# Fourth layer of a graph-network stack: full-array work and weighted values gathered into every second step

## The chip, the core and the metric

The kernel runs on one core of one Trainium2 chip. The metric is the device time of one execution in microseconds (us), lower is better. Engines are named as in the profile: PE is TensorE's matmul stream, PEld its weight loads, DVE is VectorE, ACT is ScalarE, POOL is GpSimd, and SP issues the DMAs. All data are 32-bit floats. One matmul of the program appears as two MATMUL records in the trace.

## The reference, cut to what matters

A stack of four layers works on x of 128 graphs x 64 nodes x 256 features. Each layer adds its result to x. The change touches only the fourth layer, an edge-wise attention over 512 edges with 4 heads:

```
h  = relu(layernorm(x))
Xq = (h @ W_lin.T), Xv = (h @ W_val.T)          # per head 64 wide
e  = einsum(leaky_relu(Xq[:, src] + Xq[:, dst]), a)
e  = e + log(A0[src, dst] + 1e-8)               # A0 is adj, the same for all graphs and heads
attn = softmax of e over the edges that share src
Y  = segment_sum(attn * Xv[:, dst], src)
x  = x + Y @ W_out.T
```

## The kernel before, in words

Three layers come first and take the greater part of the run; they are not touched, apart from one line of the preparation. `layer3` (L2411) is the fourth layer. x lies in SBUF as 16 blocks of 512 rows (8 graphs). A **step** g handles half a block, 4 graphs; there are 32 steps, and 8 steps make a **group** (32 graphs x 4 heads = 128 rows of attention). What follows uses a letter for each kind of PE work:

- **T**, `turned` (L2466): layer norm of the next block (`norm`, four ACT activations that write `h`), then 8 transposes into two PSUM banks. `move` (L1487) copies one bank to `hT` by DVE and the other by ACT, in turn. DVE then makes the sums `hS` that a Strassen-like product needs.
- **Q**, `queries` (L2496): 14 products of 128x256, which give `Q` and the values `V` (called `XV` in the trace). They use four banks (a, b, f, d). The second half is `rest()`; the last copies are ACT's `Q[:, 0:2]` and DVE's `Q[:, 2:4]`. `linear` (L2530) then runs `lin_p` and two reductions on DVE.
- **S**, `score` (L2545): eight products of 64x128 weights with 512 columns, each into a bank of its own. ACT applies relu to each bank, into one of eight `r` tiles.
- **R**, `reduce` (L2558): eight products that add the `r` tiles into one bank `acc` for the whole group.
- **L**: in the first step of a group, one product with a single row, `ones` by `logA`, that starts `acc` with the logarithm of the adjacency.
- **M**, `summed` (L2638), in the last step of a group: one product that adds the linear part to `acc`. `softmax` and `shifted` (L2626, L2642) are then a chain of DVE scans with an exponential on ACT. **E**, in `edgewise` (L2654): four transposes of the softmax, in step 8q+1.
- **G**, `between`/`gathered` (L2666, L2682), ten steps behind the score (`LAG`): DVE makes four `aw` tiles (five buffers), eight products of 128x64 weights write one bank, ACT copies it to `an`.
- **W**, `weighted` (L2693), one step behind G: 16 products of 64x64. DVE and ACT each copy a half to `y`.
- **O**, `output` (L2709): four products with W_out into one bank; DVE adds it to x, and SP sends it out.
- **B**, `back` (L2222), in steps 0 to 7 only: eight transposes that hand blocks 8 to 15 of the third layer's result back into x. They read `ls_t`, a tile with one buffer, whose halves DVE and ACT copy; DVE adds the two banks to x.

S uses PE as tiles of 64x128, R and G as 128x64, W as 64x64; T, Q, O, M, E and B use the full 128x128 array, and these are called **F** together. Before the change every step has the order S, W, R, G, F: T and O in even steps, Q and O in odd steps, with B in steps 0 to 7. The products S, T, Q, O, G, B and E share one pool of five PSUM banks (`l3ps`, all its tiles are called `ps`); a product into a bank waits until the reader of that bank's previous content has finished. `acc` and the output of W have banks of their own.

The order on each engine is fixed when the program is built: a scheduler interleaves the instructions of DVE and ACT, and each engine then follows its own list. Which bank and which predecessor each product gets is fixed with it. All matmuls, copies and activations have the line of a recording helper, L799, so that the trace is read by tiles. `turn` (L2571) is the end of the layer, with an order written out by hand: the last ten steps of G, W and O.

Of the kernel before, what the change touches and what calls it, by code (L numbers as in the profile page):

```python
# [8 lines left out]
F32 = mybir.dt.float32  # L9
I32 = mybir.dt.int32  # L10
AF = mybir.ActivationFunctionType
ALU = mybir.AluOpType
# [6 lines left out]
FLOOR = 1e30  # L19
# [823 lines left out]
class Plan:  # L843
# [56 lines left out]
    def rest(self):  # L900

        while any(self.queue.values()):
            for e in self.queue:
                self.fill(e, 1e9)
# [538 lines left out]
B, N, D = 128, 64, 256  # L1443
P = 128
# [3 lines left out]
E = 512  # L1448
HEADS = 4
NG = 4  # L1450
# [15 lines left out]
class Kernel:  # L1466
# [865 lines left out]
    def edges(self, w, pool, psum):  # L2332


        nc, o, io = self.nc, self.o, self.io
# [58 lines left out]
        ga = cmp[:N, :]  # L2394
        o.mul(ga, p[:N, :], self.OD[:N, :])
        p = psum.tile([P, E], F32, name="pe")
        self.mm(p[0:1, :], self.ones[:N, 0:1], ga)
        self.logA = w.tile([1, E], F32, name="ed_log")
        eps = pool.tile([1, 1], F32, name="ed_eps")
        nc.vector.memset(eps[:], 1e-8)  # L2400
        self.act(self.logA[:], p[0:1, :], AF.Ln, bias=eps[:])

        ac = self.columns(pool, "ed_ac", io["L3_gnn_a"].rearrange("h d -> (h d)"))
        self.apad = w.tile([P, 2, P], F32, name="ed_apad")
# [6 lines left out]
    def layer3(self):  # L2411
        nc, o, io = self.nc, self.o, self.io
        cx, (w,) = self.stage([("l3x", 1)], "tile")
        with cx:
            cy, pools = self.stage([("l3", 2), ("l3v", 2), ("l3s", 1), ("l3r", 6), ("l3ps", 5), ("l3cps", 1), ("l3yps", 1)], "tile")
            with cy:
                self.a02 = self.everywhere(w, "ed_a", io["L3_gnn_a"].rearrange("h d -> (h d)"))
                o.ts(self.a02[:], self.a02[:], 0.2, ALU.mult)
                self.drop, self.dropr = (w.tile([P, E], F32, name="ed_" + n) for n in ("drop", "dropr"))
                o.ts(self.drop[:], self.cont[:], 1.0, ALU.subtract, FLOOR, ALU.mult)  # L2420
                o.ts(self.dropr[:], self.contr[:], 1.0, ALU.subtract, FLOOR, ALU.mult)
                WQV = w.tile([P, 2, 2 * D], F32, name="w3_qv")
                for x, n in enumerate(("W_lin", "W_val")):
                    nc.sync.dma_start(WQV[:, :, x * D:(x + 1) * D],
                                      io[f"L3_gnn_{n}_t"].rearrange("(k p) m -> p k m", p=P))
                WO = self.weights(w, "w3_o", io["L3_gnn_W_out_t"])


                st, LAG = {}, 10
                self.turned(st, 0, *pools)  # L2430
                WQV = self.sums3(w, WQV)
                self.queries(st, 0, WQV, *pools)()
                for g in range(8 * NG):
                    v = g - LAG
                    ahead = (g + 1) // 2 if g % 2 and g + 1 < 8 * NG else None
                    self.score(st, g, *pools)
                    if v >= 1:
                        self.weighted(st, v - 1, *pools)
                    self.reduce(st, g, *pools)
                    if g % 8 == 1 and 1 < g:  # L2440
                        self.edgewise(st, g // 8 - 1, *pools)
                    if v >= 0:
                        self.between(st, v, *pools)
                    if g % 8 == 7 and g + 1 < 8 * NG:
                        self.summed(st, g // 8, *pools)
                    if g < 8:
                        self.back(8 + g, pools[4], "ps")
                    if ahead:
                        rest = self.queries(st, ahead, WQV, *pools)
                    elif g + 2 < 8 * NG:  # L2450
                        self.turned(st, g // 2 + 1, *pools)
                    if g + 6 == 8 * NG:

                        p = pools[4].tile([P, BT], F32, name="ps")
                        for c in range(4):
                            self.nc.tensor.transpose(p[:N, c * P:(c + 1) * P], self.OST[:, c, :], self.ident[:])
                        self.act_copy(self.cont[:N, :], p[:N, :])
                    if v >= 1 and g + 1 < 8 * NG:
                        self.output(st, v - 1, WO, *pools)
                    if ahead:  # L2460
                        rest()
                    if g % 8 == 7 and g + 1 < 8 * NG:
                        self.softmax(st, g // 8, *pools)
                self.turn(st, WO, pools)

# [92 lines left out]
    def reduce(self, st, g, pool, vp, sp, rp, psum, psc, psy):  # L2558


        q, i = g // 8, g % 8
        if i == 0:
            st["acc", q] = psc.tile([P, E], F32, name="acc")
            self.mm(st["acc", q][:], self.ones[0:1, :], self.logA[:], True, False)
        for fc in range(2):
            for k in range(4):
                z = 64 - 32 * (k // 2) - 4 * i
                x = 64 * (k % 2)
                self.mm(st["acc", q][x:x + 64, :], self.apad[:, fc, z:z + 64], st["r"][4 * fc + k][:], False, False)

    def turn(self, st, WO, pools):  # L2571

# [4 lines left out]
        W = [self.spread(st, v, c, *pools) for c in (0, 2)]  # L2577
        self.summed(st, q, *pools)
        e, m, m2 = self.shifted(st, q, *pools)
        self.output(st, v - 2, WO, *pools)  # L2580
        self.gathered(st, v, W, *pools)
        et = m2[:].rearrange("p (c b) -> p c b", c=4)
        p = psum.tile([P, 4, P], F32, name="ps")
        for c in range(4):
            nc.tensor.transpose(p[:, c, :], e[:, c * P:(c + 1) * P], self.ident[:])
        self.act_copy(et, p[:])
        self.weighted(st, v - 1, *pools)
        W = [self.spread(st, v + 1, 0, *pools)]
        p = psum.tile([P, P], F32, name="ps")
        for c in range(4):  # L2590
# [15 lines left out]
                o.mul(at[:, :, x, :, m, :], by(et), by(p))  # L2606
        self.gathered(st, v + 1, W, *pools)
        W = [self.spread(st, v + 2, 0, *pools)]
        self.weighted(st, v, *pools)

        late = lambda: None
        for v in range(8 * NG - 8, 8 * NG + 2):
            if v < 8 * NG:
                W.append(self.spread(st, v, 2, *pools))
            late()
            if v < 8 * NG:
                self.gathered(st, v, W, *pools)
            if v + 1 < 8 * NG:
                W = [self.spread(st, v + 1, 0, *pools)]
            if v <= 8 * NG:  # L2620
                self.weighted(st, v - 1, *pools)
            late = self.output(st, v - 2, WO, *pools, late=True)
        late()
        nc.ordered = False
# [17 lines left out]
    def shifted(self, st, q, pool, vp, sp, rp, psum, psc, psy):  # L2642

        nc, o, acc = self.nc, self.o, st["acc", q]
        e, m, m2 = (vp.tile([P, E], F32, name="sm_" + x, bufs=1) for x in ("e", "m", "m2"))
        scan = nc.vector.tensor_tensor_scan
        scan(m[:], self.drop[:], acc[:], -FLOOR, op0=ALU.add, op1=ALU.max)
        scan(m2[:, ::-1], self.dropr[:, ::-1], acc[:, ::-1], -FLOOR, op0=ALU.add, op1=ALU.max)
        o.tt(m[:], m[:], m2[:], ALU.max)
        o.sub(e[:], acc[:], m[:])  # L2650
        self.act(e[:], e[:], AF.Exp)
        return e, m, m2

# [36 lines left out]
        a = st["a", g] = vp.tile([P, 2, HEADS, N], F32, name="an")  # L2690
        self.act(a[:], A[:], AF.Copy)

    def weighted(self, st, g, pool, vp, sp, rp, psum, psc, psy):  # L2693

        a, V = st["a", g], st["V", g // 2]

        yp = psy.tile([P, 2, E], F32, name="y2")
        for m in range(2):
            for h in range(HEADS):
                for x in range(2):  # L2700
                    s, z = slice(64 * x, 64 * x + 64), slice(64 * (h % 2), 64 * (h % 2) + 64)
                    f = (2 * m + h // 2) * N
                    self.mm(yp[z, x, f:f + N], V[s, 2 * (g % 2) + m, h * N:(h + 1) * N], a[s, m, h, :])
        y = st["y", g] = vp.tile([P, 2, 2, 2, N], F32, name="y", bufs=3)
        for x in range(2):
            (self.move if g < 8 * NG - 11 else self.act_copy)(y[:, :, :, x, :].rearrange("p f m s -> p m f s"),
                      yp[:, x, 0:4 * N].rearrange("p (m f s) -> p m f s", m=2, f=2))

    def output(self, st, g, WO, pool, vp, sp, rp, psum, psc, psy, late=False):  # L2709

        y = st["y", g]
        out = self.io["out"].rearrange("b n d -> (b n) d")
        parts = []
        for lo, hi in ((0, 1), (1, 2)) if g == 8 * NG - 1 else ((0, 2),):
            p = psum.tile([P, 2, D], F32, name="ps")[:, 0:hi - lo, :]
            for m in range(lo, hi):
                for f in range(2):
                    self.mm(p[:, m - lo, :], y[:, f, m].rearrange("p x s -> p (x s)"), WO[:, f, :], f == 0, f == 1)
            parts.append((p, lo, hi))

        def add():
            for p, lo, hi in parts:
                x = self.X[g // 2][:, 2 * (g % 2) + lo:2 * (g % 2) + hi, :]
                self.o.add(x, x, p)
                self.nc.sync.dma_start(out[(2 * g + lo) * P:(2 * g + hi) * P, :].rearrange("(t p) d -> p t d", p=P), x)

        if late:
            return add
        add()
# [57 lines left out]
```

## Time and profile before

| what | value |
|---|---|
| median of 3 runs | 2326.25 us (2324.82 to 2326.69) |
| span of the profiled execution, first to last instruction | 2325.1 us |
| the median above that span | 1.15 us |
| granted TensorE clock | 0.997 |
| first S of the fourth layer | at 1755.30 us |
| last S (step 31) | at 2239.21 us |
| steps 18 and 19, S to S (2019.66 to 2053.41) | 33.75 us |
| PE busy in 1980 to 2115 us, of 135 us | 134.66 us |
| DVE and ACT busy there | 90.34 us and 55.86 us |

The profiled execution has no time of its own beside its span. A block's duration is taken from its first start to the next block's first start, since matmul ends are modelled and overlap. A PE that counts as busy can still be stretched: the same eight products of S take 3.84 us in one step and 4.91 us in another. A chain of waits names, at each step, what released an instruction last.

### The profile page before, as it was taken

The page shows a single profiled execution, that of the slowest core. Times are in us where ns is not written, and L with a number is a line of the kernel's source. Part 1 is how long each engine was busy: PE and PEld are TensorE (multiplying, and loading weights), DVE is VectorE, ACT ScalarE, POOL GpSimd, SP SyncE. Part 2 cuts the span into 40 slices and gives each one's busy share as a digit, 9 for nine tenths or more (in the row PEclk, how much of TensorE's full clock was granted, in tenths as well). Part 3 has the DMA queues.
Part 4 walks back from the last instruction along what each step waited for, and adds up shares of the span by engine and source line. Part 5 has one row for each costly group of instructions (what it writes and reads, how often), then busy time and mean ns, then how long its engine had stood idle before and what let it go on. Part 6 is the DMA issues. An engine that isn't in the chain of part 4 may idle for free.

```text
span 2325.1 us, 32725 instructions
## 1 busy us (share of the span) xinstructions
PE 2283.6 (98%) x12169; PEld 1633.1 (70%) x12169; DVE 1629.3 (70%) x4054; ACT 1139.5 (49%) x2483; POOL 3.0 (0%) x26
## 2 busy tenths in 40 slices
PE   7999998999999999999999999999999999999999
PEld 4554445676777788888999998888885544554544
DVE  8887676888447777666767676559756686766667
ACT  5765865754436654433444444336435544444321
POOL 0000000000000000000000000000000000000000
PEclk9999999999999999999999999999999999999999
DMA  5000211230000000001000002000010000000001
GB/s 171 1 1 26 65 56 30 71 83 19 1 37 0 1 19 1 1 1 37 1 1 1 1 1 73 1 1 17 1 46 28 1 5 15 15 19 14 14 24 46
DMA packets 61065, 54.81 MB, mean 24 GB/s; under 512 B 15203, under 2 KB 58724, under 8 KB 60900
## 3 DMA queue, kind: packets, MB, share of 16 engines
q1 hardware_dynamic: 60900, 52.66, 7.4%
q8 instruction: 97, 1.59, 0.3%
q14 instruction: 68, 0.56, 0.1%
HBM read 35.86 MB, written 16.78 MB: 23 GB/s over the span
## 4 chain that ended last, share of the span: by engine, by line
PE 79%; DVE 3%; issue 1%; ACT 1%; DMA 0%; SPq 0%; ACTq 0%; DVEq 0%
PE ps L799 69%; PE acc L799 5%; PE pt L799 4%; PE pe L799 1%; PE y L799 1%; DVE aw L799 1%; DVE X L799 1%; DVE sm_m L799 0%; DVE XV L799 0%; ACT ls_g L799 0%; ACT h L799 0%; DVE ls_g L799 0%; ACT big L799 0%; DVE ls_t L799 0%; DVE sm_e L799 0%
## 5 line engine op out<-in xcount | busy, mean ns | idle before, releaser
L799 ACT ACTIVATE ls_g<-ls_g,ls_b 128x512 f32<-128x512 f32 (+4 forms) x472 | 243.1, 565 | 151.4 <-DVE ls_g L799 149.6
L799 ACT ACTIVATE ls_g<-ps,ls_b 128x256 f32<-128x256 f32 (+3 forms) x268 | 115.5, 470 | 330.9 <-PE ps L799 327.7
L799 PE MATMUL ps<-z,w 128*128 128x512 f32 x512 | 254.9, 621 | 0.9 <-ACT z L799 0.9
L799 PE MATMUL ps<-big,X 128*128 128x176 f32 (+3 forms) x848 | 212.7, 366 | 0.1
L799 DVE TENSOR_TENSOR ls_g<-ls_z,ps 128x512 f32<-128x512 f32 (+5 forms) x256 | 146.8, 579 | 91.9 <-PE ps L799 90.4
L799 DVE TENSOR_TENSOR aw<-at,ed_OST 128x1024 f32<-128x1024 f32 x128 | 149.9, 1219 | 83.0 <-PE ps L799 82.8
L799 PE MATMUL ps<-ls_tx,X 128*128 128x160 f32 (+2 forms) x960 | 206.8, 326 | 0.6 <-ACT ls_g L799 0.6
L799 PE MATMUL ps<-X,X 128*128 128x160 f32 (+1 forms) x896 | 199.1, 306 | 0.0
L799 PE MATMUL ps<-X,ls_w 128*128 128x256 f32 x640 | 190.5, 379 | 0.0
L799 PEld LDWEIGHTS ps<-ls_tx,X 128*128 128x128 f32 x960 | 161.8, 190 | 15.1 <-DVE X L799 4.8
L799 PEld LDWEIGHTS ps<-big,X 128*128 128x128 f32 x848 | 145.9, 190 | 29.7 <-issue 19.4
L799 DVE TENSOR_TENSOR X<-ls_g 128x1024 f32<-128x1024 f32 (+2 forms) x108 | 117.4, 1087 | 49.9 <-ACT ls_g L799 49.8
L799 ACT ACTIVATE r<-ps 128x512 f32<-128x512 f32 x256 | 131.6, 614 | 41.5 <-PE ps L799 41.4
L799 PEld LDWEIGHTS ps<-X,X 128*128 128x128 f32 x896 | 148.4, 190 | 0.0
L799 PE MATMUL ps<-X,ls_s 128*128 128x256 f32 x480 | 142.3, 379 | 0.0
L799 PEld LDWEIGHTS ps<-z,w 128*128 128x128 f32 x512 | 87.2, 190 | 69.0 <-issue 60.2
L799 PE MATMUL ps<-ls_tx,ls_s 128*128 128x256 f32 x464 | 134.8, 379 | 0.0
L799 PE MATMUL ps<-ed_S,Q 64*128 64x512 f32 x512 | 132.9, 618 | 1.4 <-DVE hT L799 0.7
L799 PE MATMUL ps<-ls_tx,ls_w 128*128 128x256 f32 x464 | 133.2, 380 | 0.0
L799 PEld LDWEIGHTS ps<-X,ls_w 128*128 128x128 f32 x640 | 121.4, 190 | 16.8 <-DVE X L799 0.3
L799 PE MATMUL ps<-big,ls_w 128*128 128x256 f32 x464 | 131.9, 379 | 0.7 <-ACT ls_z L799 0.7
L799 PE MATMUL ps<-aw,ed_ODT 128*64 128x512 f32 x512 | 117.3, 595 | 0.1
(545 smaller groups left out, 4019.0 us busy)
## 6 DMA issues: line engine op xcount, KB each, us to landing
X<-in_x_dram SPq DMA_DIRECT2D x32, 512.0 KB
xs<-X SPq DMA_DIRECT2D x16, 512.0 KB
X<-xs SPq DMA_DIRECT2D x16, 512.0 KB
out_dram<-X SPq DMA_DIRECT2D x31, 256.0 KB
X<-in_L_gnn_Wih_t_dram SPq DMA_DIRECT2D x4, 512.0 KB
ls_w<-in_L_gnn_Wih_t_dram SPq DMA_DIRECT2D x4, 512.0 KB
ls_w<-in_L_gnn_Whh_t_dram SPq DMA_DIRECT2D x4, 512.0 KB
w<-in_L_gnn_W_t_dram SPq DMA_DIRECT2D x2, 512.0 KB
```

The source lines that it names most:

```text
L799: i = method(*a, **kw)
```

## The change

In the main loop, the full-array work F is done only after odd steps; there it holds (in steps 1, 3, 5, 7) both B, then Q, then two O, the rest of Q, and T for the block after the next. W is done only in even steps, for the two steps before, into one PSUM tile and one `y` tile (two buffers instead of three); its copies are 128x512 instead of 128x256, half as many. M and E move into F of the odd step. T of block 1 goes ahead of the loop. L is gone: `logA` is now held on all 128 partitions, the first `reduce` product of each half starts `acc`, and `shifted` begins with one DVE addition `e = acc + logA`; the scans and the subtraction then read `e` from SBUF. `turn` has three O at its start instead of one.

```
@@ preparation of the edges
-        self.mm(p[0:1, :], self.ones[:N, 0:1], ga)
-        self.logA = w.tile([1, E], F32, name="ed_log")
+        self.mm(p[:], self.ones[:N, :], ga)
+        self.logA = w.tile([P, E], F32, name="ed_log")
@@ layer3
+                self.turned(st, 1, *pools)
                 for g in range(8 * NG):
-                    v = g - LAG
-                    ahead = (g + 1) // 2 if g % 2 and g + 1 < 8 * NG else None
+                    v, odd, last = g - LAG, g % 2, g + 1 == 8 * NG
                     self.score(st, g, *pools)
-                    if v >= 1:
-                        self.weighted(st, v - 1, *pools)
+                    if last:
+                        self.weighted(st, [v - 1], *pools)
+                    elif v >= 2 and not odd:
+                        self.weighted(st, [v - 2, v - 1], *pools)
                     self.reduce(st, g, *pools)
+                    if v >= 0:
+                        self.between(st, v, *pools)
+                    if not odd or last:
+                        continue
+                    if g % 8 == 7:
+                        self.summed(st, g // 8, *pools)
                     if g % 8 == 1 and 1 < g:
                         self.edgewise(st, g // 8 - 1, *pools)
...
                     if g < 8:
-                        self.back(8 + g, pools[4], "ps")
-                    if ahead:
-                        rest = self.queries(st, ahead, WQV, *pools)
-                    elif g + 2 < 8 * NG:
-                        self.turned(st, g // 2 + 1, *pools)
+                        for i in (7 + g, 8 + g):
+                            self.back(i, pools[4], "ps")
+                    rest = self.queries(st, (g + 1) // 2, WQV, *pools)
...
-                    if v >= 1 and g + 1 < 8 * NG:
-                        self.output(st, v - 1, WO, *pools)
-                    if ahead:
-                        rest()
+                    for u in (v - 3, v - 2):
+                        if u >= 0:
+                            self.output(st, u, WO, *pools)
+                    rest()
+                    if g + 3 < 8 * NG:
+                        self.turned(st, (g + 3) // 2, *pools)
@@ reduce
-            self.mm(st["acc", q][:], self.ones[0:1, :], self.logA[:], True, False)
@@ turn
-        self.output(st, v - 2, WO, *pools)
+        for u in (v - 4, v - 3, v - 2):
+            self.output(st, u, WO, *pools)
@@ shifted
-        scan(m[:], self.drop[:], acc[:], -FLOOR, op0=ALU.add, op1=ALU.max)
-        scan(m2[:, ::-1], self.dropr[:, ::-1], acc[:, ::-1], -FLOOR, op0=ALU.add, op1=ALU.max)
+        o.add(e[:], acc[:], self.logA[:])
+        scan(m[:], self.drop[:], e[:], -FLOOR, op0=ALU.add, op1=ALU.max)
+        scan(m2[:, ::-1], self.dropr[:, ::-1], e[:, ::-1], -FLOOR, op0=ALU.add, op1=ALU.max)
         o.tt(m[:], m[:], m2[:], ALU.max)
-        o.sub(e[:], acc[:], m[:])
+        o.sub(e[:], e[:], m[:])
@@ weighted
+        yp = psy.tile([P, 2, 2, 4, N], F32, name="y2")
+        y = vp.tile([P, 2, 4, 2, N], F32, name="y", bufs=2)
+        for k, g in enumerate(gs):
...
+        n = 2 * len(gs)
         for x in range(2):
-            (self.move if g < 8 * NG - 11 else self.act_copy)(y[:, :, :, x, :].rearrange("p f m s -> p m f s"),
+            (self.move if gs[-1] < 8 * NG - 11 else self.act_copy)(y[:, :, 0:n, x, :], yp[:, x, :, 0:n, :])
```

The built order of the changed kernel is, from step 12 on, for an even step e and the odd step o after it: S(e), W (64 records in place of 32, for two steps), R, G, S(o), R, G, then F as Q, O, O, rest of Q, T, and S of the next even step right behind T.

More of the change, by code (lines that the diff above doesn't have):

```diff
@@ L2396, in edges @@
         p = psum.tile([P, E], F32, name="pe")
-        self.mm(p[0:1, :], self.ones[:N, 0:1], ga)
-        self.logA = w.tile([1, E], F32, name="ed_log")
-        eps = pool.tile([1, 1], F32, name="ed_eps")
+        self.mm(p[:], self.ones[:N, :], ga)
+        self.logA = w.tile([P, E], F32, name="ed_log")
+        eps = pool.tile([P, 1], F32, name="ed_eps")
         nc.vector.memset(eps[:], 1e-8)
-        self.act(self.logA[:], p[0:1, :], AF.Ln, bias=eps[:])
+        self.act(self.logA[:], p[:], AF.Ln, bias=eps[:])
         ac = self.columns(pool, "ed_ac", io["L3_gnn_a"].rearrange("h d -> (h d)"))
@@ L2432, in layer3 @@
                 self.queries(st, 0, WQV, *pools)()
+                self.turned(st, 1, *pools)
                 for g in range(8 * NG):
-                    v = g - LAG
-                    ahead = (g + 1) // 2 if g % 2 and g + 1 < 8 * NG else None
+                    v, odd, last = g - LAG, g % 2, g + 1 == 8 * NG
                     self.score(st, g, *pools)
-                    if v >= 1:
-                        self.weighted(st, v - 1, *pools)
+                    if last:
+                        self.weighted(st, [v - 1], *pools)
+                    elif v >= 2 and not odd:
+                        self.weighted(st, [v - 2, v - 1], *pools)
                     self.reduce(st, g, *pools)
+                    if v >= 0:
[4 more added lines that the diff above has]
+                        self.summed(st, g // 8, *pools)
                     if g % 8 == 1 and 1 < g:
                         self.edgewise(st, g // 8 - 1, *pools)
[L2442 to L2445, printed above, removed]
                     if g < 8:
-                        self.back(8 + g, pools[4], "ps")
-                    if ahead:
-                        rest = self.queries(st, ahead, WQV, *pools)
-                    elif g + 2 < 8 * NG:
-                        self.turned(st, g // 2 + 1, *pools)
-                    if g + 6 == 8 * NG:
+                        for i in (7 + g, 8 + g):
+                            self.back(i, pools[4], "ps")
+                    rest = self.queries(st, (g + 1) // 2, WQV, *pools)
+                    if g == 8 * NG - 5:
                         p = pools[4].tile([P, BT], F32, name="ps")
@@ L2457, in layer3 @@
                         self.act_copy(self.cont[:N, :], p[:N, :])
-                    if v >= 1 and g + 1 < 8 * NG:
-                        self.output(st, v - 1, WO, *pools)
-                    if ahead:
-                        rest()
-                    if g % 8 == 7 and g + 1 < 8 * NG:
+                    for u in (v - 3, v - 2):
[4 more added lines that the diff above has]
+                        self.turned(st, (g + 3) // 2, *pools)
+                    if g % 8 == 7:
                         self.softmax(st, g // 8, *pools)
@@ L2568, in reduce @@
                 x = 64 * (k % 2)
-                self.mm(st["acc", q][x:x + 64, :], self.apad[:, fc, z:z + 64], st["r"][4 * fc + k][:], False, False)
+                self.mm(st["acc", q][x:x + 64, :], self.apad[:, fc, z:z + 64], st["r"][4 * fc + k][:],
+                        i == 0 and fc == 0 and k < 2, False)
     def turn(self, st, WO, pools):
@@ L2586, in turn @@
         self.act_copy(et, p[:])
-        self.weighted(st, v - 1, *pools)
+        self.weighted(st, [v - 1], *pools)
         W = [self.spread(st, v + 1, 0, *pools)]
@@ L2608, in turn @@
         W = [self.spread(st, v + 2, 0, *pools)]
-        self.weighted(st, v, *pools)
+        self.weighted(st, [v], *pools)
         late = lambda: None
@@ L2620, in turn @@
             if v <= 8 * NG:
-                self.weighted(st, v - 1, *pools)
+                self.weighted(st, [v - 1], *pools)
             late = self.output(st, v - 2, WO, *pools, late=True)
@@ L2691, in gathered, with weighted @@
         self.act(a[:], A[:], AF.Copy)
[L2693 to L2704, printed above, removed]
+    def weighted(self, st, gs, pool, vp, sp, rp, psum, psc, psy):
+        yp = psy.tile([P, 2, 2, 4, N], F32, name="y2")
+        y = vp.tile([P, 2, 4, 2, N], F32, name="y", bufs=2)
+        for k, g in enumerate(gs):
+            a, V = st["a", g], st["V", g // 2]
+            st["y", g] = y, 2 * k
+            for m in range(2):
+                for h in range(HEADS):
+                    for x in range(2):
+                        s, z = slice(64 * x, 64 * x + 64), slice(64 * (h % 2), 64 * (h % 2) + 64)
+                        self.mm(yp[z, x, h // 2, 2 * k + m, :], V[s, 2 * (g % 2) + m, h * N:(h + 1) * N], a[s, m, h, :])
+        n = 2 * len(gs)
         for x in range(2):
-            (self.move if g < 8 * NG - 11 else self.act_copy)(y[:, :, :, x, :].rearrange("p f m s -> p m f s"),
-                      yp[:, x, 0:4 * N].rearrange("p (m f s) -> p m f s", m=2, f=2))
+            (self.move if gs[-1] < 8 * NG - 11 else self.act_copy)(y[:, :, 0:n, x, :], yp[:, x, :, 0:n, :])
     def output(self, st, g, WO, pool, vp, sp, rp, psum, psc, psy, late=False):
-        y = st["y", g]
+        y, k = st["y", g]
         out = self.io["out"].rearrange("b n d -> (b n) d")
@@ L2717, in output @@
                 for f in range(2):
-                    self.mm(p[:, m - lo, :], y[:, f, m].rearrange("p x s -> p (x s)"), WO[:, f, :], f == 0, f == 1)
+                    self.mm(p[:, m - lo, :], y[:, f, k + m].rearrange("p x s -> p (x s)"), WO[:, f, :], f == 0, f == 1)
             parts.append((p, lo, hi))
```

## The prediction

> **What bounds the kernel now.** First the page's engine line and the chain of work that ended last:
>
> ```profile
> PE 2283.6 (98%) x12169; PEld 1633.1 (70%) x12169; DVE 1629.3 (70%) x4054; ACT 1139.5 (49%) x2483; POOL 3.0 (0%) x26
> ...
> PE 79%; DVE 3%; issue 1%; ACT 1%; DMA 0%; SPq 0%; ACTq 0%; DVEq 0%
> ```
>
> PE works nearly always, and the chain is PE. So the time is the sum of the lengths of PE's blocks, and two things can change it: the number of products, and what lengthens a block without showing as idle time. I read block lengths in the timeline, from first start to first start. Steps 18 and 19, PE alone:
>
> ```profile
> 2033.90 3.97 PE L799 MATMUL ps<-ed_S,Q 64*128 64x512 f32 x16
> 2037.80 0.69 PE L799 MATMUL y<-an,XV 64*64 64x64 f32 x32
> 2038.42 3.65 PE L799 MATMUL acc<-r,ed_apad 128*64 128x512 f32 x16
> 2041.91 3.60 PE L799 MATMUL ps<-aw,ed_ODT 128*64 128x512 f32 x16
> 2045.44 1.13 PE L799 MATMUL ps<-w_qv,hT 128*128 128x256 f32 x4
> 2046.41 1.89 PE L799 MATMUL ps<-w_t,hS 128*128 128x256 f32 x8
> 2049.00 1.89 PE L799 MATMUL ps<-w_o,y 128*128 128x256 f32 x8
> ...
> 2053.41 3.91 PE L799 MATMUL ps<-ed_S,Q 64*128 64x512 f32 x16
> ```
>
> An odd step's S takes 3.90, W .62, R 3.49, G 3.53, then 7.97 for Q and O. Eight S products behind one another need about .43 each, 3.5 in all; the rest is a wait for a free bank, since ACT's relu comes every .504 ("r x8, 4.03"). In a step whose S stands directly behind T, it is longer:
>
> ```profile
> 1812.46 1.09 PE L799 MATMUL ps<-ident,ls_t 128*128 128x128 f32 x8
> 1813.15 1.28 DVE L799 TENSOR_TENSOR X<-X,ps 128x512 f32<-128x512 f32 x2 [3.91 <-PE ps L799]
> ...
> 1814.35 4.98 PE L799 MATMUL ps<-ed_S,Q 64*128 64x512 f32 x16
> 1814.66 0.58 ACT L799 ACTIVATE hT<-ps 128x512 f32<-128x512 f32 x1
> 1814.95 0.60 DVE L799 COPY ls_t<-big 128x512 f32<-128x512 f32 x1
> 1815.14 0.59 ACT L799 ACTIVATE h<-X,n_m,n_r 128x256 f32<-128x256 f32 x1
> 1815.63 0.58 ACT L799 ACTIVATE r<-ps 128x512 f32<-128x512 f32 x1
> 1816.11 0.59 ACT L799 ACTIVATE h<-X,n_m,n_r 128x256 f32<-128x256 f32 x1
> 1816.60 0.59 ACT L799 ACTIVATE r<-ps 128x512 f32<-128x512 f32 x1
> ```
>
> This S lasts 4.92, to R's start at 1819.27. ACT first copies `hT`, then alternates `h` and relu, so banks come free every .97 instead of every .50. In steps 1, 3, 5 and 7 that costs 1 us each.
>
> **What goes.** Each term is a difference of block lengths in this one execution; its span is 2325.1, 1.15 below the median of the runs (no other time of it is shown), and I add the sum to the median 2326.25.
>
> 1. L: 1.05 in steps 8, 16, 24; in step 0 it lies beside a wait for `hT`. −3.15. The four DVE additions in its place stand in the softmax chain, which has whole steps of room; in the last group 3.5 us more of O stand ahead of E.
> 2. W: the 32 records span .47 (8 groups of four, 58 ns apart) of .62, so .15 to .16 is entry and exit. Ten merged pairs: −1.6. In steps 16 and 24 W is split around L (.37 + .50), .25 more each: −.5.
> 3. F once in two steps. Leaving full-array work costs about .09 (O is 1.82 before S, 1.73 before Q), entering .06 to .10 (T .93 against .87 pure). Sixteen times .15: −2.4. The new neighbours (R or G directly before S) are not shown; the rows nearest, the last product of G (.52 for .42) and the first of S (.53 for .42), price them at what S, W, R already pay, so 0; ends −.1 and +.1 each, ±1.6 in all.
> 4. E moved into F, steps 17 and 25: R 3.59, E .59 and G 3.58 shrink by about .3: −.6. Small edges at steps 0 and 9: −.4.
> 5. S of the sixteen odd steps now follows G (or R) with no T or O before it, and with ACT free. The first relu starts 1.16 after S, then every .50; the last product waits only for the third relu, 2.75 + .06 after S, and R comes 3.77 after S. Sum 16 × 3.77 = 60.3 against 68.9 (eleven or so at 3.9, four at 4.9, 5.5 in step 9): −8.6.
>
> Together −17.3. The eviction rule of the Trainium skill speaks against 5: "TensorEngine Tiling (Array Packing)", section "PSUM Bottleneck", says that tiling speeds TensorE but not the emptying of PSUM, which may become the bottleneck. By it each S would last eight relus, 4.03, and term 5 would be −4.4, the time 4.2 later. The row of S(18), 3.84 with five banks to run ahead in, decides for the smaller price.
>
> **What comes.**
>
> 6. S of the even steps. Before, O stood between T and S:
>
> ```profile
> 2031.15 1.09 PE L799 MATMUL ps<-ident,h 128*128 128x128 f32 x8
> ...
> 2032.08 1.89 PE L799 MATMUL ps<-w_o,y 128*128 128x256 f32 x8
> ...
> 2032.28 0.60 ACT L799 ACTIVATE hT<-ps 128x512 f32<-128x512 f32 x1 [0.39 <-PE ps L799]
> 2032.77 2.06 ACT L799 ACTIVATE h<-X,n_m,n_r 128x256 f32<-128x256 f32 x4
> ```
>
> ACT had done `hT` and the four `h` (to 2034.83) when the first S product was ready for it (2035.12). Now T stands directly ahead of S in every even step up to 28, as in steps 1 to 7 above: ACT's `hT` begins about .16 after S, and in its built order the four `h` alternate with relus. The relus start 1.16, 2.13 and 3.10 after S; the product behind the third starts at 3.7 and needs 1.05 to R when it is alone (1818.21 to 1819.27). That alone makes S 4.8.
>
> A second hold: the last S products take T's banks, one of which DVE's `hT` copy frees. That copy stands in DVE's order behind the tail of Q: the last `Q` copy starts .20 after the last products of Q (2052.65), then `lin_p` .79, `XV` 1.15, the reductions .59 later, 2.42 for both: 4.95. The last Q group starts .86 + .97 before S now, so `hT` runs from 3.3 to 4.0 after S, and the product comes at 4.06: S is 5.1. The trace shows the same hold once, in step 9:
>
> ```profile
> 1867.82 0.68 DVE L799 COPY hT<-ps 128x512 f32<-128x512 f32 x1
> ...
> 1868.56 0.30 PEld L799 LDWEIGHTS ps<-ed_S,Q 64*128 64x128 f32 x4 [1.57 <-DVE hT L799]
> ```
>
> By built order the copy is late in steps 0, 4, 6, 12, 14, 20, 22, 28 (5.1 each: 40.8), earlier in 2, 8, 10, 18, 26 (4.8: 24.0); in 16 and 24 the softmax scans delay it further, about 5.8 (11.6). Sum 76.4 against 59.3 in those fifteen steps: +17.1. Bounds: 0 where R's and ACT's room hid it all, 28 if DVE made every one 5.8.
>
> 7. Second B of steps 1, 3, 5, 7. `ls_t` has one buffer, and its refill by DVE stands behind both `X` additions of the first B: the first starts B + .69 and the second ends B + 1.97 (rows above), the copy takes .60, so the second B starts at B + 2.56 instead of B + .87: 4 × 1.69 = +6.8. Below: 0 if ACT's and DVE's copies were made early. Scans in step 7: +.3.
>
> Steady F has no new stall by the rows: `aw` is five buffers ahead as before and DVE has the same work per pair of steps; the W copies are half as many, beside PE. SP's DMAs stay two in a pair, later by a step; nothing waits for them but the end, whose last ten steps keep their order.
>
> Sum: −17.3 + 17.1 + 6.8 + .3 = +6.9, so **2333**.
>
> **Rivals.** (a) *Even S isn't held*: relus keep up, banks come free as now, S stays 3.84. For it: in even steps ACT was done in time, and the pool has three banks that T doesn't use. Against it: the S of 1814.35 behind T. It gives 2333.2 − 17.1 = 2316, faster; it decides from the point where S of the even steps is below 3.95 + (17.3 − 7.1)/15 = 4.6, where gain and loss cancel with B's price kept. (b) *The second B isn't late*: `ls_t` is filled while Q's wait lasts elsewhere; 2333.2 − 6.8 = 2326, no change. (c) *VectorE later*: the `hT` copy, held by a backlog, makes almost every even S 5.8 as in 16 and 24: fifteen steps 87 against 76.4, 2340 to 2342 with the bounds of 3. For it: DVE is busy two thirds of the time and F now brings T's and Q's DVE work in one heap; against it: it has two steps to clear. That the change does not do what it says is excluded by the built order: L is absent and W's 64 records stand in a row.
>
> **How the numbers follow.** Forecast 2333, with 2329 to 2338 as its own range (term 3's ends, term 6 by .2 us a step): 62%, mostly slower (52), partly within 0.2% (10). Rival (a) 13%: faster 11, same 2. Rival (b) 10%: same 8, one each side. Rival (c) 15%: slower. Sums: faster .12, same .20, slower .68; 0.2% (4.65 us, 2321.6 to 2330.9) is about what a measurement of this kernel can tell from no change. The range goes from 2322, which leaves out most of (a), to 2342, which takes in (c).
>
> **What would show it.** In the profile after: S of even steps 4.8 to 5.1 with `h` rows between the relus of ACT and weight loads waiting for DVE `hT`; odd S about 3.8; the second B 2.5 us behind the first; no row of `ones` by `ed_log`; W in 64 records of about 1.1. If even S is near 3.9, or the second B follows at .9, terms 6 or 7 were wrong; if odd S is near 4.0, term 5 was; if R, G and W blocks are longer beside their new neighbours, term 3 was.

## The result and the profile after

The changed kernel takes 2343.29 us (median of 5 runs, 2339.79 to 2346.30) against 2326.25 (median of 5 runs, 2324.82 to 2329.14): ratio 1.0064, 95% interval 1.0051 to 1.0077. It is **slower by 17 us**; the forecast was 7 us slower. The ratio stands for 15 us (12 to 18 by its interval), less than the quotient of the two medians, 1.0073: the kernel before, run again on four later occasions (7 to 29 executions each), had medians of 2327.72 to 2328.45, 1.5 to 2.2 above the five here. The profiled execution of the changed kernel has a time of 2346.30 and a span of 2344.5, 19.4 longer than the span of before. The page's engine line:

```profile
PE 2294.2 (98%) x12161; PEld 1645.4 (70%) x12161; DVE 1629.4 (70%) x4048; ACT 1139.5 (49%) x2473; POOL 2.9 (0%) x26
```

DVE and ACT are as busy as before, to 0.1 us, PE has eight records fewer, and its busy time is 10.6 us longer. The chain of waits is PE's again, 80% for 79%. Nothing in these views names a cause: PE's blocks have become longer inside. So the whole layer was added up by kind of block, start to start, from the first T (1742.89 before, 1746.57 after) to the last O (2317.82 and 2337.28):

| blocks of the fourth layer | predicted, us | before, after | measured |
|---|---|---|---|
| L (term 1) | -3.15 | 3.15, 0 | -3.15 |
| W (term 2) | -2.1 | 13.62, 11.54 | -2.08 |
| T, Q, O, E, G, start and tail (terms 3 and 4) | -3.4 | 300.50, 297.46 | -3.04 |
| R | 0 | 112.89, 115.05 | +2.16 |
| S of odd steps (term 5) | -8.6 | 68.89, 66.70 | -2.19 |
| S of even steps 0 to 28 (term 6) | +17.1 | 59.24, 76.78 | +17.54 |
| B (term 7, with the 0.3 of step 7) | +7.1 | 7.38, 13.91 | +6.53 |
| sum, with unlisted blocks that did not change | +6.9 | 574.94, 590.72 | +15.8 |

The 3.7 us that the span has beyond these lie ahead of the layer, where the granted clock between 100 and 200 us was 0.97 in this execution and 1.00 in that of before. A kernel below with the same code up to there (both O behind T) starts the layer at 1741.25 with a clock of 0.998, so they are not the change's. The five spans of the changed kernel go from 2338.0 at a clock of 0.998 to 2344.5 at 0.995.

**An even S after** (step 14, timeline; T ends, S begins):

```profile
1962.17 1.04 PE L799 MATMUL ps<-ident,h 128*128 128x128 f32 x8
...
1963.14 5.24 PE L799 MATMUL ps<-ed_S,Q 64*128 64x512 f32 x16
1963.24 0.60 ACT L799 ACTIVATE hT<-ps 128x512 f32<-128x512 f32 x1 [2.00 <-PE ps L799]
...
1964.04 2.43 DVE L799 TENSOR_REDUCE lin<-lin_p 64x16 f32<-64x1024 f32 x2
1964.30 0.60 ACT L799 ACTIVATE r<-ps 128x512 f32<-128x512 f32 x1
1964.79 0.59 ACT L799 ACTIVATE h<-X,n_m,n_r 128x256 f32<-128x256 f32 x1
...
1966.51 0.69 DVE L799 COPY hT<-ps 128x512 f32<-128x512 f32 x1
...
1968.30 1.16 PE L799 MATMUL y<-an,XV 64*64 64x64 f32 x64
```

S lasts 5.16, from 1963.14 to W at 1968.30. ACT does `hT`, then `h` and relu in turn; DVE's `hT` copy, which frees a bank, comes 3.4 us after S began, behind the two reductions: the row that the forecast built by hand. The second B, in the waits view and in the timeline of step 1:

```profile
PEld ps L799 <- DVE ls_t L799: 6.8, 4, 1.7
```
```profile
1776.49 1.28 DVE L799 TENSOR_TENSOR X<-X,ps 128x512 f32<-128x512 f32 x2 [10.40 <-PE ps L799]
...
1777.69 0.61 DVE L799 COPY ls_t<-big 128x512 f32<-128x512 f32 x1
...
1778.36 1.09 PE L799 MATMUL ps<-ident,ls_t 128*128 128x128 f32 x8 [1.47 <-DVE ls_t L799]
```

The columns of the first are the total, the times and the longest: four waits of at most 1.7 us, 6.8 in all; the first B began at 1775.80, so the second is 2.56 behind it.

**What was not foreseen** is step 9:

```profile
1876.61 3.35 DVE L799 RECIPROCAL sm_m<-sm_m 128x512 f32<-128x512 f32 x1
...
1876.90 2.99 PE L799 MATMUL ps<-ed_S,Q 64*128 64x512 f32 x12
...
1878.12 0.60 ACT L799 ACTIVATE r<-ps 128x512 f32<-128x512 f32 x1 [2.50 <-PE ps L799]
...
1878.73 1.28 ACT L799 ACT_TABLE_LOAD   x1
...
1881.82 0.20 ACT L799 ACTIVATE n_y<-n_v 128x4 f32<-128x4 f32 x1 [1.80 <-DVE n_v L799]
1881.93 2.53 ACT L799 ACTIVATE r<-ps 128x512 f32<-128x512 f32 x5
1882.56 0.98 PEld L799 LDWEIGHTS ps<-ed_S,Q 64*128 64x128 f32 x4 [3.50 <-ACT r L799]
```

In ACT's fixed order, layer norm's square root `n_y` with its table load stands behind the first relu of S. Its input `n_v` comes from DVE, which is in the softmax's reciprocal until 1879.96 and does six smaller operations before `n_v` starts at 1881.61. For 3.8 us no relu starts, the five banks fill, and PE's weight loads wait 3.50 us. S takes 8.15, R behind it 5.68 (before: 5.50 and 3.77).

### The profile page after: what moved, and what is told of

Read it like the earlier page. It is cut to its first block, busy times and chain, and to the rows that moved or that the text cites. A ratio compares the mean times of both kernels' runs of the same rounds, so it can differ in the third digit from the quotient of the medians.

```text
span 2344.5 us, 32706 instructions
## 1 busy us (share of the span) xinstructions
PE 2294.2 (98%) x12161; PEld 1645.4 (70%) x12161; DVE 1629.4 (70%) x4048; ACT 1139.5 (49%) x2473; POOL 2.9 (0%) x26
## 4 chain that ended last, share of the span: by engine, by line
PE 80%; DVE 3%; ACT 1%; issue 1%; DMA 0%; ACTq 0%; DVEq 0%; SPq 0%
PE ps L799 69%; PE acc L799 5%; PE pt L799 4%; PE pe L799 1%; PE y L799 1%; DVE X L799 1%; DVE sm_m L799 0%; ACT ls_g L799 0%; ACT h L799 0%; DVE lin L799 0%; DVE ls_t L799 0%; DVE aw L799 0%; DVE ls_g L799 0%; DMA ed_a<-in_L_gnn_a_dram 0%; DVE XV L799 0%
## 5 line engine op out<-in xcount | busy, mean ns | idle before, releaser
L799 PE MATMUL ps<-ed_S,Q 64*128 64x512 f32 x512 | 146.7, 627 | 2.9 <-ACT r L799 2.7
L799 PE MATMUL acc<-r,ed_apad 128*64 128x512 f32 x512 | 119.5, 608 | 0.0
```

Source lines behind the costliest of these rows:

```text
L799: i = method(*a, **kw)
```

## Experiments

Theory A: an even S is held twice, by ACT's `h` among the relus and behind that by the bank that DVE's `hT` copy frees late. B: ACT alone. C: T directly ahead of S costs PE by itself. The three kernels are the changed one, each with an order added (`hold` puts what follows behind a given instruction in the built order of its engine; all diffs below are shortened):

```diff
 # late_h: ACT's four h behind the relus of the even step
+        self.nc.hold((None, None, behind))      # behind = last relu of the even S
         for j in range(TPB):
             self.act(h[:, j, :], self.X[i][:, j, :], AF.Relu, ...)
+        self.nc.hold()
 # early_hT: linear called behind T, ordered behind DVE's hT copy
-            self.linear(st, i, ...)              # at the end of rest()
+                    nc.hold((None, st["copied"], None))
+                    self.linear(st, (g + 1) // 2, *pools)
+                    nc.hold()
 # both_orders: both edits
```

> The changed kernel, with ACT's four h activations ordered behind the eight relus of the even step's S; nothing else. Theory A (the even S is held twice: first by ACT, which alternates h and relu, and behind that by T's bank, which DVE's hT copy frees late): the relus come every .50, but S stays near 5.1 in the steps 0, 4, 6, 12, 14, 20, 22, 28 and 5.8 in 16 and 24, where the bank is late anyway; only 2, 8, 10, 18, 26 fall from 4.8 to about 3.9. The sum of the fifteen falls by about 4, the time by about 4 us. Theory B (ACT alone holds it): all fifteen fall to about 3.9, the time by 15 to 17 us. Theory C (T directly ahead of S costs PE by itself, whatever ACT and DVE do): no change.

> The changed kernel, with DVE's lin_p and its two reductions ordered behind the hT copy of T; nothing else. Theory A: T's bank is free about 1.2 us after S begins, and what is left is ACT's alternation: all fifteen even S about 4.8, the sum falls from 76.8 to 72, the time by 4 to 5 us. Theory B (ACT alone): no change in S. Theory C: no change.

> The changed kernel with both orders: h behind the relus on ACT, linear behind the hT copy on DVE. Theory A: fifteen even S of 3.85 to 3.9, sum 58 in place of 76.8, the time 16 to 19 us lower: far more than the two single edits add up to (8 to 9), since either hold suffices. Theory B: the same as late_h. Theory C: no change in S.

| kernel | fifteen even S, us | odd S, us | layer without its start, us | time, us |
|---|---|---|---|---|
| before | 59.24 | 68.89 | 562.5 | 2326.25 |
| changed | 76.78 | 66.70 | 577.9 | 2343.29 |
| late_h | 74.62 | 67.86 | 575.8 | 2343.57 |
| early_hT | 70.78 | 67.84 | 572.8 | 2339.74 |
| both_orders | 59.27 | 71.25 | 564.9 | 2332.15 |

(The start, up to the first S, is left out of the fourth column: it was 12.78 in the profiles of the changed kernel and of best, and 11.2 in seven others that have the same work there. The kernel before, run beside the last three, took 2328.45; their ratios to it are 1.0070, 1.0050 and 1.0017.) Alone the edits give 2.2 and 6.0 us of even S, together 17.5. B and C fall, A stands. Its sum for late_h was missed by half: S of step 2 rose to 5.17, 18 and 26 are 4.21, and S of step 9 grew to 9.31; the layer is 2.1 shorter and the time no lower. Step 14 of late_h, timeline:

```profile
1960.71 3.91 PE L799 MATMUL ps<-ed_S,Q 64*128 64x512 f32 x14
...
1961.87 3.53 ACT L799 ACTIVATE r<-ps 128x512 f32<-128x512 f32 x7 [0.46 <-PE ps L799]
...
1964.08 0.69 DVE L799 COPY hT<-ps 128x512 f32<-128x512 f32 x1
...
1964.82 1.12 PE L799 MATMUL ps<-ed_S,Q 64*128 64x512 f32 x2 [0.21 <-DVE hT L799]
```

Seven relus run in a row, and the last product still waits for `hT`; S is 5.17 as in the changed kernel. The same step of both_orders:

```profile
1955.06 3.91 PE L799 MATMUL ps<-ed_S,Q 64*128 64x512 f32 x16
...
1956.22 4.03 ACT L799 ACTIVATE r<-ps 128x512 f32<-128x512 f32 x8 [0.46 <-PE ps L799]
```

S is 3.84. But the time fell by 11, not 16 to 19: S of steps 9 and 17 is now 8.25 and 7.12, with `n_y` and its table load ahead of six or more of the relus, and that of 25 is 4.53.

**O as cover.**

```diff
-                    for u in (v - 3, v - 2): ... self.output(st, u, ...)
                     rest()
                     if g + 3 < 8 * NG:
                         self.turned(st, (g + 3) // 2, *pools)
+                    for u in (v - 3, v - 2): ... self.output(st, u, ...)
```

> The changed kernel, with both O after T instead of between the halves of Q. From step 14 on 3.6 us of O then stand between T and S, as 1.8 did before the change. Theory A: S of steps 14 to 28 falls from 41.3 in all to 8 x 3.85 = 30.8, the time by about 10 us; the second half of Q does not wait (in steps 1 to 5, where no O stands there, its 28 records take 6.05 as they do around O). Rival: the second half of Q waits for DVE's sums without O ahead of it, Q grows from 6.15 by 0.5 to 1 us in each odd step, and half of the gain is gone.

S of steps 14 to 28 fell to 36.1, half of what was expected, and Q did not grow (92.80 against 92.44): the rival named the wrong place. In step 20 the weight loads of S wait for DVE's `hT` (0.57) and twice for DVE's addition to X (0.42 each): O brings banks that DVE, late, has to free, in place of T's. S of 17, 25 and 30 grew by 0.5, 0.4 and 0.7. The layer without its start is 574.3 in the profile, 3.7 shorter, but the time, 2342.75 (2335.82 to 2347.41), is that of the changed kernel.

**The second B.**

```diff
-                        for i in (7 + g, 8 + g):
-                            self.back(i, pools[4], "ps")
+                        self.back(7 + g, pools[4], "ps")
                     rest = self.queries(...)
                     ...
                     rest()
+                    if g < 8:
+                        self.back(8 + g, pools[4], "ps")
```

> The changed kernel, with the second B of steps 1, 3, 5 and 7 between the second half of Q and T, in place of directly behind the first B; nothing else. Theory A (the second B waits for ls_t, which has one buffer and whose refill by DVE stands behind the first B's additions): the two B take 0.9 each, 1.8 in place of 3.48 in each of the four steps, the time falls by 6 to 7 us. Rival (DVE and ACT are behind as a whole there, and the wait is only shown at B): the same time is lost in the S or R that follow, and the layer changes by less than 2 us.

B fell from 13.91 to 7.16 as expected, and the time to 2336.49. But the layer without its start (570.4) has more in it: S of 9 is 3.90 here and R 3.59, 6.3 less, since the built order had moved `n_y` away; against it S and R of steps 2, 4, 6 and 8 grew, by 5.6 in all, where DVE's additions to X come late: in step 2 they start 2.3 and 2.9 us after S. (In best, below, they start 1.0 and 0.4 ahead of it, and S is 3.84.) Both theories hold in part.

**The square root among the relus.** Both orders, and:

```diff
+        nc.hold((None, None, root))              # root = last relu of an odd S
         self.act(y[:], v[:], AF.Sqrt)
+        nc.hold()
```

> The kernel with both orders (h behind the relus, linear behind the hT copy), and ACT's square root of layer norm, n_y, ordered behind the relus of the odd step's S. Theory A (S of steps 9, 17 and 25 is held since n_y stands among the relus in ACT's order and waits for DVE, which is in the 3.35 us reciprocal of the softmax): S of 9, 17 and 25 falls from 8.25, 7.12 and 4.53 to about 3.9, R of 9 and 17 from 5.28 and 4.24 to 3.5 or 3.6; the layer is 10 us shorter than with both orders alone (576.1), the time about 2322. Rival (ACT's two loads of a function table, 1.28 us each, hold it): they stay in these steps, and S of 9 stays above 5.

S of 9, 17 and 25 became 3.90, 4.53 and 4.53, R of 9 and 17 3.59 and 3.48. The layer is 567.8, 8.3 shorter than with both orders (B of step 1, 4.57 for 3.50, took 1.1 of what was expected, Q of step 9 0.8, and S of 25 did not fall), the time 2324.91. Step 9, timeline:

```profile
1865.85 3.97 PE L799 MATMUL ps<-ed_S,Q 64*128 64x512 f32 x16
...
1866.90 3.35 DVE L799 RECIPROCAL sm_m<-sm_m 128x512 f32<-128x512 f32 x1
1867.07 4.03 ACT L799 ACTIVATE r<-ps 128x512 f32<-128x512 f32 x8 [1.54 <-PE ps L799]
```

The reciprocal lies beside S as before, and S doesn't notice. The table load moved together with `n_y`, so this run doesn't part the two; in the rows of step 9 above the load has 1.28 us of the gap and the wait for `n_v` 1.80. The 0.63 left in 17 and 25 is ACT's copy to `y`, which waits there for DVE's, behind the reciprocal; the first relu of step 17 follows 1.84 us after S (1990.21):

```profile
1987.15 3.35 DVE L799 RECIPROCAL sm_m<-sm_m 128x512 f32<-128x512 f32 x1
...
1990.42 0.63 DVE L799 COPY y<-y 128x512 f32<-128x512 f32 x1
...
1991.08 0.60 ACT L799 ACTIVATE y<-y 128x512 f32<-128x512 f32 x1 [5.78 <-DVE y L799]
```

**Terms 1 and 2 alone, on the kernel before** (F in every step; only L out, only W paired, and both), and L put back into the changed kernel:

```diff
 # l_only: reduce and shifted of the changed kernel      # l_back: those of before
 # w_only: weighted of the changed kernel, called as
+                    elif v >= 2 and g % 2 == 0:
+                        self.weighted(st, [v - 2, v - 1], *pools)
 # gains: both
```

> The kernel before, with L taken out (DVE adds the logarithm) and W done for two steps in every second one, as in the changed kernel, but with F in every step as before. By the sum's terms 1 and 2, L -3.15 and W -2.1: the layer falls from 574.9 to about 569.7, the time by 5 us (0.2%), with S, R, G, T, Q, O and B as before. Rival (the DVE addition or the larger y copies cost elsewhere): some S or R becomes longer, and less than 2 us remain.

> The kernel before, with L alone taken out: the logarithm is added by DVE at the head of the softmax chain. Theory D (the addition makes the chain later, so that ACT's exponential or square root, which stands among the relus of S in steps 8, 9, 16, 17, 24, 25, is waited for): L -3.15, but S of 16, 24 and 25 grows by 0.7 to 1.5 each, as it did where both parts were done (5.77, 4.92, 4.92), and 0 to 1 us of the gain remains. Rival (the larger W and y copies did that, the addition is free): S stays at 4.25, 4.25 and 3.90, the layer falls from 574.9 by 3 us.

> The kernel before, with W alone done for two steps in every second one; L stays. Theory D: W -1.6 to -2.1 is kept, S as before but for the steps 16 and 24, where W was split; the layer falls from 574.9 by about 2. Rival (the larger W and y copies spoil S): S of 16, 24 or 25 grows by 0.7 or more, and the layer does not fall.

> The changed kernel with L put back and DVE's addition taken out; the rest of the change stays. Theory D (the addition in the softmax chain moves ACT's exponential and square root in among relus, and DVE's hT copy later): L costs 3.15 in steps 8, 16 and 24 again, but S of step 9 (8.15) and R (5.68) fall by 3 us or more together, S of 16 and 24 (5.79) by 0.5 to 0.7 each, so that the layer is 1 to 3 us shorter than the changed kernel's 590.7, its start of 12.78 left aside. Rival (step 9 is held by B's and Q's work of step 7 on DVE whatever the chain holds): S of 9 stays above 7, and the layer is 2 to 3 us longer.

| kernel | layer, us | ratio to before (95%) |
|---|---|---|
| gains | 575.1 (before 574.9) | 0.9996 (0.9983 to 1.0010) |
| l_only | 576.7 | 1.0012 (1.0003 to 1.0022) |
| w_only | 574.4 | 0.9996 (0.9986 to 1.0006) |
| l_back | 587.9 (changed 590.7, of which 1.5 start) | 1.0061 (1.0044 to 1.0077) |

Taking L out is worth -3.15 in its own row and makes the kernel before a little slower (0.12%): S of 16, 24 and 25 is 5.78, 4.92 and 5.12 (before 4.25, 4.25, 3.90). With both parts done S is 5.0 longer in all, and nothing is left of the 5 us expected. Step 16 of the kernel before, and of l_only, timelines:

```profile
1981.40 0.68 DVE L799 TENSOR_TENSOR sm_e<-acc,sm_m 128x512 f32<-128x512 f32 x1
...
1982.11 0.63 ACT L799 ACTIVATE sm_e<-sm_e 128x512 f32<-128x512 f32 x1 [3.54 <-DVE sm_e L799]
```
```profile
1984.35 0.69 DVE L799 TENSOR_TENSOR sm_e<-sm_e,sm_m 128x512 f32<-128x512 f32 x1
1984.51 0.60 ACT L799 ACTIVATE r<-ps 128x512 f32<-128x512 f32 x1 [2.18 <-PE ps L799]
...
1985.12 1.28 ACT L799 ACT_TABLE_LOAD   x1
...
1986.42 0.63 ACT L799 ACTIVATE sm_e<-sm_e 128x512 f32<-128x512 f32 x1
...
1986.95 3.51 ACT L799 ACTIVATE r<-ps 128x512 f32<-128x512 f32 x7
```

DVE's addition made the input of the exponential later (its subtraction is at 1984.35, 1.0 after S began; before, at 1981.40, 2.4 ahead of S), and the exponential and its table load now stand behind the first relu: 1.8 us without relus. W alone kept 1.33 in its row, and 0.6 of it in the layer; R of step 17, 3.90, took 0.3. In the changed kernel, L put back costs its 3.15 and returns 3.9 in S and R of step 9: the time is the same. S of 24, which D expected shorter, is 6.20 for 5.79. Theory D stands in the main, and taking L out gained nothing in either kernel.

**All edits together**: best is late_ny with the second B apart; best2 also has the softmax's exponential behind the relus of the even step.

```diff
-                    if g % 8 == 7:                       # in best2, after the next even S:
-                        self.softmax(st, g // 8, *pools)
+                        nc.hold((None, None, st["relus"]))
+                        self.softmax(st, late, *pools)   # late = the group just ended
+                        nc.hold()
```

> The changed kernel with all four edits: h behind the relus, linear behind the hT copy, n_y behind the odd step's relus, and the second B between Q and T. If the three holds are all that spoiled the change, the layer is 576.1 - 10 - 6.6 = 559.5, 15 us shorter than the kernel before (574.9), the time about 2312, ratio 0.9935. If ACT's exponential, which in its built order stands ahead of the last relu of step 8, waits there for DVE, S of step 8 is some us longer.

> The kernel with all four edits, and the softmax's exponential ordered behind the eight relus of the following even step. If ACT's exponential, waiting for DVE among the relus of step 8, made R there 5.04, R becomes 3.58 and the layer 1.4 us shorter than 563.2. If instead DVE's later chain now holds E in step 9, E, or Q behind it, grows by as much, and nothing is won. S of 17 and 25, 4.53 since ACT's y copy waits there for DVE behind the reciprocal, stays or grows.

best takes 2318.49 (ratio 0.9951, 0.9934 to 0.9967), best2 2316.26 (0.9950, 0.9935 to 0.9964). In best, R of step 8 is 5.04, with ACT's exponential waiting for DVE ahead of the last relu; in best2 it is 3.58, S of 17 and 25 are 3.90, against what was expected, and only S of 9 grew, to 4.43: without the start its layer is 2.2 shorter than that of best, which the times can't tell from no change. Its layer is 559.5, 15.5 shorter than before (of which 1.2 is the start): the change, with its orders mended, is worth about **11 us** on this kernel (0.5%, by the interval 0.36 to 0.65%). As it was made it costs 15 to 17. What the same kind of orders would give the kernel before was not tried; its S of steps 1, 3, 5, 7, 9, 10 and 11 are 7.4 us longer together than the 3.90 and 3.84 of undisturbed steps, so part of the 11 may be had without the change.

## Why the prediction was right in its direction and too small

The layer became 15.8 longer, not 6.9: of the 8.9 between, 6.4 is term 5 and 2.2 is R, to which the prediction gave nothing. The time of 2343.29 lies above 2338, and 1.3 above 2342, the end that was to take in rival (c); by the ratio it is 2341. Rival (c)'s own numbers, 2333.2 + 87 − 76.4, give 2343.8 and not "2340 to 2342", so that the measured time comes near to it by chance: even S was as forecast.

- **Terms 6 and 7** were right in mechanism, place and size (+17.54 for +17.1, +6.53 for +7.1). By steps: 5.16 to 5.17 in 4, 6, 14, 20, 22, 28 (5.1 forecast), 5.39 in 0 and 12, 4.81 in 2, 8, 10, 18 (4.8), 5.79 in 16 and 24 (5.8). Only 26, 4.21, was over-priced: there, as in 28, no `h` stands among the relus, and the relus come every .48. The runs on the two orders show that both holds are needed to explain it.
- **Term 5** failed: "Sum 16 × 3.77 = 60.3". Fifteen of the odd S take 3.90 to 3.95: the first relu starts 1.22 after S, not 1.16, and the last product stands 1.05 ahead of R, not 0.96. That costs 2.0, and both were in rows that the prediction quotes or uses (2035.12 in step 19, 1.05 in term 6).
- The rest of term 5, 4.4, and the 1.9 of R, is step 9. The prediction read S as limited by relus and banks, and gave ACT nothing else to do in odd steps ("with ACT free"). It had looked at ACT's built order in even steps and not in step 9, although S was 5.50 there before, a row that it put into its sum as if the edit removed it.
- The rule of the Trainium skill that was weighed there ("TensorEngine Tiling (Array Packing)", "PSUM Bottleneck") would have made each odd S 4.03; measured is the middle between it and 3.77. In the even S and in step 9 PE did wait for banks to be emptied, as the page warns; but what made it wait was the order of ACT's and DVE's other work, for with both orders set the relus came every .50 and S was 3.84.
- **Term 1** has the right row, and the sentence on its cover, "the softmax chain, which has whole steps of room", is the false one. E has room; ACT's exponential and square root, which wait for that chain in a fixed order among the relus, do not.
- **Terms 2 and 3**: -2.08 for -2.1, and -3.04 for -3.4 with 4. R or G directly before S costs no more: R stays 3.48 to 3.59 but in 2, 4 and 6 (3.94, 3.64, 3.64) and in 9, G 3.53.
- **Rival (c)**, DVE later, named the right engine and the wrong place: not all even S at 5.8, but one odd S at 8.15, where ACT waits for DVE.

Left open: the medians differ by 17.0, the ratio stands for 15, and the layer differs by 15.8, of which 0.4 is the start (12.41 and 12.78); 1 to 3 us go to executions whose granted clock differs, and weren't settled.

## What to carry to other kernels

Before work is moved, write down for each engine the order in which it will run, and look in it for an instruction that waits for a slow neighbour ahead of the ones that empty PSUM; one such row, `n_y` among the relus of step 9, made S and R there 4.6 us longer than before the change, more than the three removed products of L gained (3.15). Two holds on the same block must be undone together: each undone alone gave 2 and 6 us, both 17.5. When an operation goes from the bound engine to a chain on an engine with idle time, ask what is queued in order behind the chain's end, not whether the chain's last reader has room.

## What was not expected of the hardware

At the start of the layer PE pauses three times in the changed kernel, for 0.78, 0.35 and 2.27 us (0.60 us of work between 1750 and 1752). Its granted clock then was 0.50 from 1754 to 1756, and the records of Q stood 0.43 us apart in place of 0.22. In both_orders, with the same three pauses, the clock stayed at 1.00; in the kernel before, with pauses of 0.78 and 1.07 only, it was 0.54 from 1745 to 1750. What decides it was not tried.
